# Second stage of a four-layer network: VectorE's range, spread, statistics and mean in another order

## The chip, the cores and the metric

The kernel runs on one core of a Trainium2 chip. The metric is the device time of one execution in microseconds, quoted as the median of several runs.

PE is TensorE (PEld its weight loads), DVE is VectorE, ACT is ScalarE, POOL is GpSimd and SP is the engine that issues transfers.

## The reference

Four layers, each `x = x + conv(groupnorm(x))`, on 8192 samples of 8 x 16 x 16. The second stage of the kernel is the end of layer 1 and the start of layer 2:

```python
# --- layer 1 ---
x = x + _L1_conv_ref(_gn(x), ...)      # ends with batch norm over all samples, then relu
# --- layer 2 ---
x = x + _L2_conv_ref(_gn(x), ...)      # starts with sx = 127 / max(abs(_gn(x))) over all samples
def _gn(v, G=4, eps=1e-5):
    ...
    m = jnp.mean(g, axis=(2, 3, 4), keepdims=True)
    s = jnp.var(g, axis=(2, 3, 4), keepdims=True)
    return ((g - m) / jnp.sqrt(s + eps)).reshape(v.shape)
```

Batch norm needs all of y first, and the quantizer of layer 2 needs the largest normalized value of all samples. Between the two stands a pass over 64 tiles of 128 x 2048 f32 (1.049 MB): load x and y, add relu(a y + b) to x, find the group statistics of each sample, subtract the mean, find the largest absolute value, store x again (but for the last ten tiles, which stay on chip).

## The kernel before

Engines that are wrapped in `InOrder` execute in the order of the program: `pe, dve, act, pool = (InOrder(tc, e) for e in (...))`. So the order of the calls in the last loop is the order of instructions on each engine.

```python
    def sums_pe(ps, x, sq):                       # PE: sums of x and of x*x over channels of a group
        for k, src in ((0, x), (1, sq)):
            for q in range(NQ):
                pe.matmul(ps[32 * q:32 * q + 32], L["wsum"][:, k], src[:, q * BANK:(q + 1) * BANK],
                          start=(k == 0), stop=(k == 1))
# ... cut ...
        def sum2(t):
            x, y = T[t]["x"], T[t].pop("y")
            act.activation(y, y, AF.Relu, bias=bn_b, scale=bn_a)
            pool.tensor_tensor(x, x, y, ALU.add)

        def sums2(t):                             # ACT, then PE
            sq = p2.tile([P, F], F32, name=f"sq2_{t}", tag="sq2", bufs=2)
            act.activation(sq, T[t]["x"], AF.Square)
            ps = ps2.tile([P, BANK], F32, name=f"gs_{t}", tag="gs")
            sums_pe(ps, T[t]["x"], sq)
            T[t]["ps"] = ps

        def stats2(t):                            # DVE: s_c, psc, gnst, sq_c, gnst; then POOL: power -0.5
            stats_small(gnst[:, t], psc[:, 32:64], T[t].pop("ps"), f"c{t}")
            stats_pow(gnst[:, t])

        def spread2(t):                           # DVE: diag_b, rows_c; then PE: gb
            ps = ps2.tile([P, 2, P], F32, name=f"gb_{t}", tag="gb")
            rows = to_rows(diag[t % 2], psc[:, 0:NQ], [gnst[:, t]], f"c{t}")
            for k, sel in enumerate((L["sel0"], L["sel1"])):
                pe.matmul(ps[:, k], sel, rows, start=True, stop=True)
            T[t]["gb"] = ps

        def centre2(t):                           # DVE: x - mean (mean in gb); then the store
            # ... two halves: x = x - gb[:, 0] ...
            if t >= NT - KEEP:
                kept[t] = x
            else:
                nc.sync.dma_start(x2_d[t], x)

        def range2(t):                            # DVE: max |x|, times 1/deviation (in gb), max
            # ... top = max |x| in two halves; top = top * gb[:, 1]; amax[:, t] = max(top) ...

        for t in range(NT + 3):
            on(t + 3, lambda t: t < 3 or load2(t))
            on(t, sum2)
            on(t - 2, spread2)
            on(t - 1, sums2)
            on(t - 3, range2)
            on(t - 2, centre2)
            on(t - 1, stats2)
```

The lines of the profile name the tiles of this loop. `gs` holds PE's sums and `s_c` is the first operation of the statistics, which reads them; `gnst` holds mean and 1/deviation; `diag_b` and `rows_c` are the two VectorE operations of the spread, and `gb` its result from PE; `top` belongs to the range. Below, PE's burst is its work for one tile without a pause: the spread of t-2, then the sums of t-1.

## Time and profile before

| | before |
|---|---|
| time, median of 3 | 4309.59 us (4309.05 to 4310.04) |
| the second stage (until the next stage's first VectorE work) | about 2985 to 3535 us |
| time per tile in it | 8.25 us |
| busy in 3100 to 3400: VectorE, PE, GpSimd | 83%, 55%, 67% |
| granted PE clock, DMA share, DMA rate there | 0.65, 1.00, 382 GB/s |

The page's table of 40 slices shows the stage as a hole in the PE row. Each digit is the busy share of one slice in tenths; a slice of the kernel before is 108 us long.

```profile
PE   6999999999999999999999999996555549999999
DVE  6666666666666666666666666655888879999997
PEclk9999999999999999999999999998666669999999
DMA  3222222222222222222222222114999933444442
```

In slices 29 to 32 PE falls to 5, its clock to 6 and DMA rises to 9, while VectorE is at 8. The stage is some 550 us, an eighth of the time.

### The profile page before, as it was taken

The page shows a single profiled execution, that of the slowest core. Times are in us where ns is not written, and L with a number is a line of the kernel's source. Part 1 is how long each engine was busy: PE and PEld are TensorE (multiplying, and loading weights), DVE is VectorE, ACT ScalarE, POOL GpSimd, SP SyncE. Part 2 cuts the span into 40 slices and gives each one's busy share as a digit, 9 for nine tenths or more (in the row PEclk, how much of TensorE's full clock was granted, in tenths as well). Part 3 has the DMA queues.
Part 4 walks back from the last instruction along what each step waited for, and adds up shares of the span by engine and source line. Part 5 has one row for each costly group of instructions (what it writes and reads, how often), then busy time and mean ns, then how long its engine had stood idle before and what let it go on. Part 6 is the DMA issues. An engine that isn't in the chain of part 4 may idle for free. (4 is left out here: it accounts for less than half of the span.)

```text
span 4309.0 us, 51166 instructions
## 1 busy us (share of the span) xinstructions
PE 3972.4 (92%) x19804; PEld 2087.4 (48%) x19866; DVE 3158.7 (73%) x4892; ACT 2153.1 (50%) x1606; POOL 2692.6 (62%) x1428
## 2 busy tenths in 40 slices
PE   6999999999999999999999999996555549999999
PEld 3555555555555555555555555553111115555555
DVE  6666666666666666666666666655888879999997
ACT  3444444444444444444444444443444437777776
POOL 5655546556555555455565565534666648999999
PEclk9999999999999999999999999998666669999999
DMA  3222222222222222222222222114999933444442
GB/s 116 88 98 80 106 88 88 108 79 88 108 79 94 103 80 102 94 88 108 79 89 108 79 90 106 69 52 171 391 382 382 382 123 137 176 186 186 176 186 108
DMA packets 80595, 587.26 MB, mean 136 GB/s; under 512 B 8928, under 2 KB 9056, under 8 KB 9184
## 3 DMA queue, kind: packets, MB, share of 16 engines
q1 hardware_dynamic: 80064, 583.04, 35.3%
q8 instruction: 156, 2.56, 0.2%
q10 hardware_dynamic: 288, 0.94, 0.1%
q14 instruction: 87, 0.71, 0.0%
HBM read 326.00 MB, written 257.95 MB: 136 GB/s over the span
## 5 line engine op out<-in xcount | busy, mean ns | idle before, releaser
L43 PE MATMUL po<-u,core 128*128 128x512 f32 x4096 | 1934.4, 608 | 0.0
L43 ACT COPY u<-pu 128x2048 f32<-128x2048 f32 x512 | 955.6, 1866 | 1052.3 <-PE pu L43 1052.3
L43 POOL TENSOR_TENSOR v<-x1n 128x256 f32<-128x256 f32 (+1 forms) x768 | 562.0, 761 | 907.1 <-issue 557.9
L43 PEld LDWEIGHTS po<-u,core 128*128 128x128 f32 x4096 | 722.8, 190 | 816.2 <-issue 815.2
L43 POOL TENSOR_TENSOR mvb<-mvb,mhalf 128x64 f32<-128x64 f32 (+1 forms) x67 | 676.1, 10093 | 127.4 <-DVE mvb L43 127.4
L43 PE MATMUL pu<-w,xn 32*128 32x256 f32 x8192 | 590.4, 402 | 11.3 <-DVE xn L43 9.3
L43 PEld LDWEIGHTS pu<-w,xn 32*128 32x128 f32 x8192 | 371.9, 185 | 311.7 <-issue 210.4
L43 ACT ACTIVATE sq<-x 128x2048 f32<-128x2048 f32 x192 | 366.2, 1907 | 268.8 <-POOL x L43 268.7
L43 DVE TENSOR_TENSOR x<-po,x 128x512 f32<-128x512 f32 x256 | 177.1, 692 | 420.0 <-PE po L43 412.4
L43 ACT ACTIVATE m<-pm,b 128x256 f32<-128x256 f32 x256 | 121.3, 474 | 591.7 <-PE pm L43 576.9
L43 DVE TENSOR_TENSOR y<-m,pm 128x256 f32<-128x256 f32 x512 | 192.9, 419 | 183.0 <-ACT m L43 183.0
L43 POOL TENSOR_TENSOR mv<-mv,mhalf 128x4 f32<-128x4 f32 x128 | 130.7, 1021 | 311.0 <-DVE mv L43 311.0
L43 POOL TENSOR_TENSOR x<-x,yl 128x2048 f32<-128x2048 f32 x64 | 290.6, 4540 | 10.5 <-ACT yl L43 10.4
L43 POOL TENSOR_TENSOR x<-x,w 128x2048 f32<-128x2048 f32 x64 | 289.9, 4531 | 11.4 <-DMA x<-in_xt 6.0
L43 PE MATMUL gb<-rows_c,sel 128*128 128x128 f32 x256 | 72.7, 436 | 237.8 <-DVE rows_c L43 237.8
L43 POOL TENSOR_TENSOR lo<-t,hi 128x2048 fp32r<-128x2048 f32 x64 | 273.4, 4272 | 19.4 <-POOL mv L43 16.2
L43 PE MATMUL pc<-v,fast 128*128 128x256 f32 x1024 | 275.3, 390 | 3.9 <-DVE y L43 3.9
L43 PE MATMUL pm<-v,fast 128*128 128x256 f32 x1024 | 264.8, 381 | 0.0
L43 PEld LDWEIGHTS pm<-v,fast 128*128 128x128 f32 x1024 | 195.1, 191 | 133.4 <-issue 118.6
L43 POOL TENSOR_TENSOR x<-x,c 128x2048 f32<-128x2048 f32 x64 | 236.6, 3697 | 0.0
L43 PE MATMUL pf<-hi,sign 128*128 128x512 f32 x768 | 226.9, 433 | 0.0
L43 PE MATMUL pf<-lo,sign 128*128 128x512 f32 x768 | 219.5, 423 | 3.4 <-ACT lo L43 3.4
(176 smaller groups left out, 5434.7 us busy)
## 6 DMA issues: line engine op xcount, KB each, us to landing
x_d<-x SPq DMA_DIRECT2D x118, 1024.0 KB, 4.7
x<-x_d SPq DMA_DIRECT2D x118, 1024.0 KB, 6.9
xb<-in_xb SPq DMA_DIRECT2D x64, 1024.0 KB, 4.8
x<-in_xt SPq DMA_DIRECT2D x64, 1024.0 KB, 4.8
y_d<-y SPq DMA_DIRECT2D x64, 1024.0 KB, 4.1
yl<-y_d SPq DMA_DIRECT2D x64, 1024.0 KB, 9.2
out_dram<-x SPq DMA_DIRECT2D x64, 1024.0 KB, 3.8
w<-in_pack ACTq DMA_DIRECT2D x1, 690.0 KB, 9.4
```

The costliest lines, as they stand in the source:

```text
L43: return self.tc.keep_in_program_order(op(*args, **kwargs))
```

## The change

The intent: in the kernel before, VectorE waits 1.13 us per tile for GpSimd's power, because the spread, which needs the power, follows the statistics, which start it, at once. With the mean and the range put between, the power should run unseen.

```diff
         for t in range(NT + 3):
             on(t + 3, lambda t: t < 3 or load2(t))
             on(t, sum2)
+            on(t - 3, range2)
             on(t - 2, spread2)
             on(t - 1, sums2)
-            on(t - 3, range2)
+            on(t - 1, stats2)
             on(t - 2, centre2)
-            on(t - 1, stats2)
```

## The prediction

> **What bounds the kernel now.** I read the page's 40 slices first: DMA is at 9 in only a few slices, and those are the stage that the change touches. So I cut that stage out with the table by windows. Its columns are the window and its length, then busy us (and instructions) of PE, PEld, DVE, ACT and POOL, then the granted PE clock, the DMA share and GB/s.
>
> ```profile
> core 0: us, PE busy (x) PEld busy (x) DVE busy (x) ACT busy (x) POOL busy (x), PEclk, DMA share, GB/s
> 3020.00:3040.00 20.00, 9.44 (x48) 2.67 (x40) 16.51 (x33) 11.00 (x6) 11.87 (x6) 0.74 1.01 422
> ...
> 3440.00:3460.00 20.00, 10.49 (x52) 3.08 (x44) 17.05 (x33) 10.45 (x6) 11.88 (x5) 0.67 1.00 387
> ...
> 3490.00:3500.00 10.00, 5.83 (x28) 1.53 (x20) 8.63 (x16) 5.34 (x3) 5.80 (x3) 0.67 0.00 0
> ```
>
> The reader is to see that DMA looks full (share 1.00) and still is not the bound. VectorE is 82 to 86% busy with the transfers (17.05 of 20; 16.51 of 20) and 86% without them (8.63 of 10, DMA share 0.00). The statistics' reduction s_c starts at 3194.54, 3202.79 and 3211.03 in mid-stage and at 3491.38, 3499.62 and 3507.87 after the last load: 8.25 us per tile both times. A tile moves 3 x 1.049 MB, which at 8.25 us is 381 GB/s; just after the start the same mix ran at 422. So the pace is a loop among engines. The timeline of one tile shows it (start, duration, engine, operation, and in brackets the idle time before):
>
> ```profile
> 3202.79 0.69 DVE L43 TENSOR_REDUCE s_c<-gs 128x32 f32<-128x512 f32 x1
> ...
> 3204.16 0.16 DVE L43 SCALAR_TENSOR_TENSOR gnst<-psc,sq_c 128x4 f32<-128x4 f32 x1
> 3204.40 1.02 POOL L43 TENSOR_TENSOR gnst<-gnst,mhalf 128x4 f32<-128x4 f32 x1 [2.72 <-DVE gnst L43]
> ...
> 3205.45 0.19 DVE L43 TENSOR_TENSOR diag_b<-gnst,psc 128x32 f32<-128x32 f32 x1 [1.13 <-POOL gnst L43]
> 3205.68 0.31 DVE L43 STREAM_TRANSPOSE rows_c<-diag_b 128x128 f32<-128x128 f32 x1
> 3205.91 2.30 DVE L43 TENSOR_REDUCE top<-x 128x64 f32<-128x1024 f32 x2
> ...
> 3206.14 1.19 PE L43 MATMUL gb<-rows_c,sel 128*128 128x128 f32 x4 [3.48 <-DVE rows_c L43]
> ...
> 3208.77 2.34 DVE L43 TENSOR_TENSOR x<-x,gb 128x1024 f32<-128x1024 f32 x2
> 3208.97 1.94 PE L43 MATMUL gs<-sq,wsum 128*32 128x512 f32 x8
> ...
> 3211.03 0.68 DVE L43 TENSOR_REDUCE s_c<-gs 128x32 f32<-128x512 f32 x1
> ```
>
> In start-to-start times the loop is: statistics with its gap 1.57 (3202.79 to 3204.36), wait for GpSimd's power 1.09, spread 0.46 (3205.45 to 3205.91), range 2.86 (to 3208.77), mean 2.26 (to 3211.03). The sum is 8.24. VectorE's only wait is the power; that is the wait the change aims at. The second thing to see is hidden: PE starts on the spread only when the rows are ready (3205.99), does the spread and then the sums for the next statistics, and ends at 3208.97 + 1.94 = 3210.91, just 0.12 before s_c starts. That run of matmuls is covered now by range and mean, 5.12 us of VectorE work, almost exactly its own length. The waits table of 3000 to 3500 says the same:
>
> ```profile
> PE gb L43 <- DVE rows_c L43: 223.3, 60, 4.3
> ...
> DVE diag_b L43 <- POOL gnst L43: 67.9, 60, 1.1
> DVE s_c L43 <- PE gs L43: 18.4, 2, 17.2
> ```
>
> VectorE waits for the power 60 times, and for PE's sums only twice, both at the stage's start.
>
> **What the Trainium skill says.** "TensorE: Matmul & The Clock Gate", section on the array's architectural detail (engine queue depths): VectorE, ScalarE and GpSimd queues are strict FIFO; PE may pull weight loads ahead, but, says the section on what happens when a matmul is issued, the matmuls keep program order. The trace agrees: in all 64 tiles the sums follow the spread, though their inputs were ready earlier (x of 3208's sums was added before 3197). The same page, part 1 on the clock gate: PE is at half clock until about 3.4 us of activity. The trace agrees: granted 0.50 in every window from 3197.2 to 3209, and the bursts (first gb to the end of the sums) take 4.76 us cold and 3.94 to 4.7 when the clock rises inside them; the mean of 64 is 4.52. "DMA: Bandwidth & Descriptors", section on where 436 GB/s comes from, gives about 358 GB/s as the limit of HBM per core; the trace differs, 381 sustained and 422 at the start, so I do not use that limit.
>
> **The change part by part.** No instruction is added or removed; per tile one order of VectorE work becomes another. Before: spread(t-2), range(t-3), mean(t-2), statistics(t-1). After: range(t-3), spread(t-2), statistics(t-1), mean(t-2). PE still has spread(t-2), then sums(t-1).
>
> 1. Gain: the power of t-1 now starts ahead of mean and range, 2.26 + 2.86 = 5.12 us of work that does not need it. GpSimd has finished the preceding addition long before (3201.68 against 3204.40). The 1.09 us wait goes.
> 2. Loss: between the rows of t-2 and the statistics of t-1 VectorE has nothing left in its program. The statistics need PE's sums, these stand behind the spread, and the spread needs the rows that VectorE has just made. The mean of t-2 could run after 1.2 us of spread, but stands behind the statistics in a FIFO. So VectorE waits for the full burst: handing over rows to PE 0.06 to 0.15 (the starts at 3008.26 and 3206.14 after rows ended at 3008.20 and 3205.99; I take 0.10), burst 4.52, PE's end to s_c 0.08 (3013.03 to 3013.11). That is 4.70.
> 3. New loop, all on the path: range 2.86 + diagonal and transpose to its end 0.54 + wait 4.70 + statistics 1.57 + mean 2.26 = 11.93 us, against 8.24. Net +3.69 per tile.
>
> The stage's start already has one such case: for the second tile nothing of range was there to cover PE, and rows ended at 3008.20, s_c came at 3013.11, 4.91 us later at cold clock.
>
> Whole stage: the second tile's statistics start at 3013.11 as now. The last (62 tiles on) start at 3013.11 + 62 x 11.93 = 3752.8. Then come statistics 1.57, mean 2.26, range 2.86, rows 0.54, last spread alone 0.10 + 0.70, mean 2.26, range 2.86, together 13.15: 3765.9. Before, the next stage began its first VectorE work at 3535.5. The difference is 230 us; before and after the stage nothing changes. 4309.6 + 230 = 4540.
>
> Other limits are far off at 11.93: GpSimd has 4.54 + 1.02, ScalarE 2.08 + 1.91 a tile, DMA 3.146 MB in 7.5 us at 422 GB/s. The centred tile is stored later in its turn, but loads are asked for three tiles ahead (36 us) and took a median of 9 to landing.
>
> **The rivals.**
> A. As intended: the power's wait goes and nothing replaces it. The loop falls to 7.15, but the stores and loads then need 7.45 at the start's 422 GB/s. 64 x (0.8 to 1.1) gives 50 to 70 us: 4240 to 4260, which is still within 2%. For it: the 60 waits of 1.13. Against: it needs sums(t-1) ready when VectorE asks, and PE's order forbids that.
> B. DMA is the bound (share 1.00), so nothing moves: 4310. Against: the same pace without DMA at 3490 to 3530. And even a DMA-bound stage would be overtaken by a loop of 11.9.
> C. PE's burst, now on the path, runs warm. At 3019.2 to 3021.2 the granted clock was 0.87 and eight sums took about 1.3 instead of 1.94. With spread at 0.7 and twice 1.3 less overlap the burst would be some 3.0, the loop 10.4: +135, 4445. Against: PE would idle 7.4 us a tile instead of 3.5, which does not keep a clock up. If instead every burst is cold (4.77), the loop is 12.18 and the time 4556.
>
> **Range and chances.** The main step is a chain of dependences, not a rate, so slower is nearly sure. The size hangs on the burst, between some 4.3 and 4.8, and on 0.1 us of handing over: 4540, with 4505 to 4575 for 8 in 10. Faster by over 2% (under 4223) is out of reach even for A: 0.01. Within 2% would need A or B: 0.03. Slower: 0.96.
>
> **What would show it.** Step 1: the wait of diag_b for the power vanishes from the waits table. Step 2: s_c waits for PE's gs some 60 times, about 4.7 each, near 290 us. Step 3: s_c of neighbouring tiles lie 11.9 apart, VectorE's share in the stage falls from 84% to about 58%, DMA's to near 265 GB/s (3.146 MB in 11.93 us), and the stage lasts some 230 us longer. The number of instructions and their durations stay. The prediction would be wrong if PE ran the sums ahead of the spread, if the burst ran warm (C), or if a wait I do not see, such as of the mean for the spread's buffers, came on top.

## The result, and the profile after

The changed kernel takes 4543.28 us (median of 4; 4542.78 to 4544.1) against 4309.82 for the kernel before beside it. The ratio is 1.0542 (95% interval 1.0523 to 1.056).

The waits of the changed kernel from 3000 to 3740 us (engine and tile that waited, what it waited for, us in total, times, longest):

```profile
PE gb L43 <- DVE rows_c L43: 452.5, 62, 7.4
...
DVE s_c L43 <- PE gs L43: 310.6, 62, 17.4
...
ACT yl L43 <- DMA yl<-y_d: 4.2, 3, 2.4
DVE diag_b L43 <- POOL gnst L43: 1.1, 1, 1.1
```

The wait that the change aimed at is gone: diag_b waits for GpSimd once in place of 60 times. In its place VectorE waits for PE's sums in every tile: without the first wait of 17.4 us, which the kernel before has too, 61 waits take 293 us, 4.81 each. The timeline of one tile shows the order that makes them:

```profile
3301.25 0.69 DVE L43 TENSOR_REDUCE s_c<-gs 128x32 f32<-128x512 f32 x1 [4.62 <-PE gs L43]
...
3302.71 2.35 DVE L43 TENSOR_TENSOR x<-x,gb 128x1024 f32<-128x1024 f32 x2
3302.87 1.02 POOL L43 TENSOR_TENSOR gnst<-gnst,mhalf 128x4 f32<-128x4 f32 x1 [6.26 <-DVE gnst L43]
...
3304.98 2.34 DVE L43 TENSOR_REDUCE top<-x 128x64 f32<-128x1024 f32 x2
...
3307.88 0.18 DVE L43 TENSOR_TENSOR diag_b<-gnst,psc 128x32 f32<-128x32 f32 x1
3308.09 0.31 DVE L43 STREAM_TRANSPOSE rows_c<-diag_b 128x128 f32<-128x128 f32 x1
...
3308.55 1.19 PE L43 MATMUL gb<-rows_c,sel 128*128 128x128 f32 x4 [7.37 <-DVE rows_c L43]
...
3311.38 1.94 PE L43 MATMUL gs<-sq,wsum 128*32 128x512 f32 x8
...
3313.38 0.69 DVE L43 TENSOR_REDUCE s_c<-gs 128x32 f32<-128x512 f32 x1 [4.98 <-PE gs L43]
```

The power (3302.87) now lies beside the mean and the range. But PE idles for 7.37 us until the rows are there, then works from 3308.55 to 3313.32 while VectorE stands still. The two engines take turns. The table by windows for 3100 to 3400 us, first of the kernel before, then of the changed kernel (columns as in the prediction):

```profile
3100.00:3400.00 300.00, 165.83 (x737) 53.70 (x736) 250.49 (x473) 140.60 (x73) 201.82 (x73) 0.65 1.00 382
```

```profile
3100.00:3400.00 300.00, 114.45 (x500) 38.11 (x500) 174.04 (x327) 97.36 (x50) 139.09 (x52) 0.57 0.77 263
```

VectorE falls from 250 to 174 of 300 us, DMA from 382 to 263 GB/s. The stages around it have not changed: the stage before it ends within 1 us of where it did, and the stage behind it lasts 773 us in both traces (3535.5 to 4309.0, and 3769.0 to 4542.3).

### The profile page after: what moved, and what is told of

Same layout as the page of the kernel before. It is cut to its first block, busy times and chain, and to the rows that moved or that the text cites. A ratio compares the mean times of both kernels' runs of the same rounds, so it can differ in the third digit from the quotient of the medians.

```text
span 4542.3 us, 51154 instructions
## 1 busy us (share of the span) xinstructions
PE 3977.7 (88%) x19804; PEld 2091.0 (46%) x19866; DVE 3159.2 (70%) x4892; ACT 2152.8 (47%) x1606; POOL 2691.0 (59%) x1428
## 5 line engine op out<-in xcount | busy, mean ns | idle before, releaser
L43 PEld LDWEIGHTS gb<-rows_c,sel 128*128 128x128 f32 x256 | 59.4, 322 | 565.3 <-issue 551.1
L43 POOL TENSOR_TENSOR gnst<-gnst,mhalf 128x4 f32<-128x4 f32 x64 | 65.2, 1019 | 407.7 <-DVE gnst L43 407.7
L43 DVE TENSOR_REDUCE s_c<-gs 128x32 f32<-128x512 f32 x64 | 44.3, 691 | 320.2 <-PE gs L43 320.2
```

Of the source, the lines that this page charges most:

```text
L43: return self.tc.keep_in_program_order(op(*args, **kwargs))
```

## The experiments

**Theory:** the order of the program exposes PE's burst (spread of t-2, then sums of t-1) between the rows and the statistics. In the kernel before, range and mean covered it. **First rival:** the mean now comes last in its turn, so the store comes late, and the transfers set the pace. For it speaks that a store of x took a median of 10.1 us to land in the stage after the change, and 4.8 before. **Second rival:** PE's granted clock fell from 0.65 to 0.57, and slow matmuls alone cost the time.

| run | VectorE's order, PE's order | time, us | ratio to before (95% interval) | per tile, us |
|---|---|---|---|---|
| before | spread, range, mean, statistics; spread, sums | 4310.9 | 1 | 8.25 |
| after | range, spread, statistics, mean; spread, sums | 4543.3 | 1.0542 (1.0523 to 1.056) | 11.95 |
| e1 | range, spread, mean, statistics; spread, sums | 4402.6 | 1.0213 (1.0196 to 1.023) | 9.72 |
| e2 | spread, range, statistics, mean; spread, sums | 4365.1 | 1.0125 (1.011 to 1.0141) | 9.10 |
| e3 | as after; sums, spread | 4250.2 | 0.9861 (0.9846 to 0.9875) | 7.29 |
| e4 | as before; sums, spread | 4310.6 | 0.9999 (0.9984 to 1.0014) | 8.24 |
| e5 | as after; spread twice, sums | 4579.9 | 1.0625 (1.0608 to 1.0643) | 12.54 |
| e6 | as before; spread twice, sums | 4329.0 | 1.0045 (1.003 to 1.006) | 8.53 |
| e7 | as after; spread, sums, 12 idle matmuls | 4604.6 | 1.0683 (1.0666 to 1.0701) | 12.80 |
| e8 | as after; spread, sums, 7 idle matmuls | 4416.1 | 1.0245 (1.0228 to 1.0263) | 9.90 |

The last column is the mean distance of the starts of s_c from the second tile to the last. All runs gave correct results. The time of "after" is from other rounds than e1 to e8; the kernel before had 4309.7 to 4310.9 us in all of them.

### e1: the range alone goes ahead

```diff
+            on(t - 3, range2)
             on(t - 2, spread2)
             on(t - 1, sums2)
-            on(t - 3, range2)
             on(t - 2, centre2)
             on(t - 1, stats2)
```

> One part of the change alone: the range of t-3 goes ahead of the spread of t-2, mean and statistics stay as before. Theory (VectorE's program must cover PE's burst of spread and sums): the wait for the power goes (range lies between), but only the mean, 2.26 us, and not range and mean, 5.12 us, is left to cover the burst. Loop = range 2.86 + rows 0.54 + (0.10 + burst 4.55 + 0.08) + statistics 1.57 = 9.60 us, against 8.25: 62 x 1.35 = +84 us, about 4394. Inside: the mean waits some 1.4 us for the spread, the statistics some 1.0 us for the sums. Rival (the late mean delays the stores and so the transfers, the mean stays early here): no loss, 4310 or less. Rival (less PE work per time lowers PE's clock and that alone costs): the same sign as the theory but no predicted size.

Measured: 4402.6 us and 9.72 us per tile, where 4394 and 9.60 were expected. VectorE in one tile:

```profile
3202.91 0.31 DVE L43 STREAM_TRANSPOSE rows_c<-diag_b 128x128 f32<-128x128 f32 x1
3204.66 2.35 DVE L43 TENSOR_TENSOR x<-x,gb 128x1024 f32<-128x1024 f32 x2 [1.43 <-PE gb L43]
3208.20 0.69 DVE L43 TENSOR_REDUCE s_c<-gs 128x32 f32<-128x512 f32 x1 [1.19 <-PE gs L43]
```

Both waits are those that were forecast: 1.43 us for the spread and 1.19 for the sums, 1.06 on average. The 0.12 us that are missing in the expected loop are the burst (mean 4.63, not 4.55) and the handing over from rows to PE (0.15, not 0.10). The mean is early here, and still the tile takes 1.5 us longer: the first rival does not explain this run.

### e2: the statistics alone go ahead of the mean

```diff
             on(t - 2, spread2)
             on(t - 1, sums2)
             on(t - 3, range2)
+            on(t - 1, stats2)
             on(t - 2, centre2)
-            on(t - 1, stats2)
```

> The other part alone: the statistics of t-1 go ahead of the mean of t-2, the range stays behind the spread. Theory: the power is covered by the mean (2.26 us), and the burst is covered by the range only (2.86 us). Loop = rows 0.54 + (0.10 + 4.52 + 0.08) + statistics 1.57 + mean 2.26 = 9.07 us: 62 x 0.82 = +51 us, about 4361. VectorE waits some 1.8 us per tile for the sums, none for the power. Rival (late mean delays the stores): the whole loss of the change shows here, about 4540, since the mean is as late as there.

Measured: 4365.1 us and 9.10 us per tile; VectorE waited 127 us for the sums in 63 waits, 2.02 each, and for the power once. The waits from 3000 to 3480 us, with the stage's first of 17.0 us:

```profile
DVE s_c L43 <- PE gs L43: 122.6, 53, 17.0
...
DVE diag_b L43 <- POOL gnst L43: 1.1, 1, 1.1
```

The mean comes as late here as in the changed kernel, and the time is 178 us lower: a late store is not the cause. The two parts alone cost 92 and 54 us, together 146, and the whole change 233. They do not add up, because both part runs save the same 1.09 us wait for the power, which can be saved only once: in us per tile, 1.47 + 0.85 + 1.09 = 3.41 of the 3.70. The remaining 0.3 is the slack of the kernel before. In the two part runs range and mean together hide 5.12 us, which is more than one burst with its handing over. The traces show the excess: PE's sums ended 0.38 us ahead of s_c on average in the kernel before, and 0.07 in the changed one, a difference of 0.31.

### e3: the change, with PE's sums ahead of the spread

```diff
             on(t - 3, range2)
-            on(t - 2, spread2)
             on(t - 1, sums2)
+            on(t - 2, spread2)
             on(t - 1, stats2)
             on(t - 2, centre2)
```

> The change with one swap on PE: sums of t-1 ahead of the spread of t-2 (range, sums, spread, statistics, mean). Theory: the sums need nothing of the rows, so PE can do them during range; the statistics find them done, the mean finds the spread done or nearly so. VectorE's loop is then its own work, 2.86 + 0.46 + 1.57 + 2.26 = 7.15 us, and the transfers may bind at 3.146 MB / 422 GB/s = 7.45 us: 62 x (7.45 - 8.25) = -50 us, about 4260 (4242 if DMA keeps up). s_c waits for PE no more. Rival (late mean, late stores): the mean is as late as in the change, so about 4540. Rival (PE's clock): PE has the same work, so no gain over the change of this size.

Measured: 4250.2 us, 293 us under the changed kernel and 61 under the kernel before. This is the fastest version. VectorE's order, with the mean behind the statistics, is that of the change to the last call. Two calls are swapped, and only PE sees it (ScalarE's square keeps its place). That settles the first rival. In the windows 3100 to 3200 and 3440 to 3460 of this run:

```profile
3100.00:3200.00 100.00, 61.33 (x272) 17.79 (x272) 95.07 (x182) 54.33 (x28) 75.32 (x29) 0.62 1.01 427
...
3440.00:3460.00 20.00, 11.99 (x60) 3.57 (x59) 19.33 (x36) 7.22 (x4) 12.06 (x5) 0.67 0.01 1
```

VectorE is 95% busy and DMA moves 427 GB/s, for which a tile's 3.146 MB take 7.37 us. Behind the last load the tiles follow each other in about 7.1 us, VectorE's own work, as the start-to-start sum of 7.15 said. In mid-stage both limits lie so close together that a tile takes between 7.0 and 8.7 us, and a load of x takes a median of 16.7 us to land (7.2 before). ScalarE waits 188 us in all for loads of y there (4.2 us in the kernel before). So the gain stops at the transfers.

### e4: the kernel before with PE's orders swapped, a control

```diff
-            on(t - 2, spread2)
             on(t - 1, sums2)
+            on(t - 2, spread2)
             on(t - 3, range2)
             on(t - 2, centre2)
             on(t - 1, stats2)
```

> Control: the kernel before with the same swap on PE alone, VectorE's order untouched. Theory: VectorE waits for the power, not for PE, so the loop stays 8.25 us and the time about 4310 (4300 to 4315). If PE's burst already set the pace before (it ends only 0.12 us ahead of the statistics), this would be faster by some tens of us.

Measured: 4310.6 us, no difference. In the kernel before, the power's wait sets the pace and PE's burst is covered; freeing PE alone gives nothing. Of the orders tried, only both edits together gain.

### e5 and e6: a dose of PE work in the burst

In both kernels each spread is computed twice, which lengthens the burst and changes no other instruction.

```diff
-            for k, sel in enumerate((L["sel0"], L["sel1"])):
-                pe.matmul(ps[:, k], sel, rows, start=True, stop=True)
+            for _ in range(2):
+                for k, sel in enumerate((L["sel0"], L["sel1"])):
+                    pe.matmul(ps[:, k], sel, rows, start=True, stop=True)
```

> Dose of PE's burst in the changed kernel: the two matmuls of every spread are issued twice (same result). One spread took 1.12 us to the first sum. Theory (burst stands openly between rows and statistics): +1.12 us in each of 63 loops, +71 us, about 4614; if the longer burst lets the clock rise inside it, less, down to some +45 us. VectorE's wait for the sums grows by the same amount. Rival (late mean and stores set the pace): nothing to +5 us, about 4545.

> The same dose in the kernel before. There range and mean cover 5.04 us from the end of the rows to the statistics; 0.10 + (4.52 + 1.12) + 0.08 = 5.82 us would be needed. Theory (the cover was nearly used up): the sums come 0.78 us late, +49 us, about 4360 (a rise of the clock inside the burst: down to +25 us), and a wait of the statistics for PE appears that the kernel before does not have. Rival (PE is far from mattering in the kernel before, 55% busy in the stage): about 4311, unchanged.

Measured: 4579.9 and 4329.0 us. Both signs are the theory's and both sizes are below the ranges that I gave: +37 us where at least +45 was expected, and +18 where at least +25 was. The dose was smaller than I thought. One tile of e5:

```profile
3310.01 2.04 PE L43 MATMUL gb<-rows_c,sel 128*128 128x128 f32 x8 [7.36 <-DVE rows_c L43]
3311.99 1.63 PE L43 MATMUL gs<-x,wsum 128*32 128x512 f32 x8
3313.44 1.03 PE L43 MATMUL gs<-sq,wsum 128*32 128x512 f32 x8
```

Two spreads take 1.98 us to the first sum, only 0.86 more than one; and in this longer burst the clock has risen when the last eight sums run (1.03 us in place of 1.94). The mean burst grew from 4.59 to 5.17 us, and 62 x 0.58 = 36 us is the loss that was measured. In e6 the mean burst is 4.90 and the tiles alternate: a burst of 4.40 gives 8.25 us per tile, one of 5.40 gives 8.82. So the cover of the kernel before ends at 5.40 - (8.82 - 8.25) = 4.83 us, and its cold burst of 4.76 was just inside. The wait of the statistics for PE that was forecast for e6 is there, behind every second tile: 31 waits of some 0.5 us, besides the one at the stage's start.

### e7 and e8: PE kept busy in its idle time

```diff
             sums_pe(ps, T[t]["x"], sq)
+            for _ in range(7):                       # 12 in e7
+                pe.matmul(idle, L["sel0"], core01.rearrange("p s n -> p (s n)")[:, 0:512], start=True, stop=True)
```

`idle` is a PSUM tile that nobody reads.

> How much of the open burst is the low clock: the changed kernel with twelve matmuls of 128x512 on constants behind each tile's sums, in PE's 7.4 us of idle time, into a bank nobody reads (the result is unchanged). At full clock they should take some 12 x 0.47 = 5.7 us (1934 us / 4096 in the first stage), so they end before the next rows. Theory (order exposes the burst, and idle time makes it cold): the granted clock rises towards 1.0, the burst falls from 4.59 to about 3.0 and the loop from 11.95 to about 10.4, 62 x 1.6 = 99 us less than the change: about 4445, and still 3% over the kernel before, because the order still exposes the burst. Rival (the low clock is the whole cause of the loss): back to about 4310. If the clock does not rise, the twelve matmuls take 11 us and the time rises well over 4543.

> As e7, with seven idle matmuls in place of twelve: in e7 each counted as two records and took 0.87 us at full clock, so twelve took 10.4 us and themselves filled the loop (12.80 us), while the granted clock rose to 1.00 and the burst fell to 2.46 us. Seven take 6.1 us and fit in the 7.4 us between the sums' end and the next spread. Theory: burst stays at 2.46, the loop is 2.86 + 0.54 + (0.10 + 2.46 + 0.08) + 1.57 + 2.26 = 9.87 us, 62 x 2.08 = 129 us under the change: about 4414, still 104 us (2.4%) over the kernel before. Rival (the low clock is the whole cause): about 4310. If 1.3 us of idle time per loop lets the clock fall again: near 4540.

e7 measured 4604.6 us. I had misread a count: an f32 matmul is two records in the trace, so twelve took 10.4 us and not 5.7, and they delayed the spread themselves. But PE ran at a granted clock of 1.00 and the burst fell to 2.46 us. e8 with seven measured 4416.1 us where 4414 was expected:

```profile
3301.48 6.28 PE L43 MATMUL idle<-core,sel 128*128 128x512 f32 x14
3308.92 0.68 PE L43 MATMUL gb<-rows_c,sel 128*128 128x128 f32 x4 [1.16 <-DVE rows_c L43]
3309.53 1.06 PE L43 MATMUL gs<-x,wsum 128*32 128x512 f32 x8
3310.42 1.04 PE L43 MATMUL gs<-sq,wsum 128*32 128x512 f32 x8
```

The burst is 2.54 us at clock 1.00, and VectorE still waits 2.75 us for the sums. So the second rival holds a part: the exposed burst alone costs 106 us at full clock (4416.1 - 4309.8), and the low clock, which comes from PE's idling, makes it 233. But the fall of the clock from 0.65 to 0.57 is not what costs it. The burst took 4.52 us on average in the kernel before already, and 4.59 after, which is 62 x 0.07 = 4 us. The change exposed a burst that was slow before. In e3 the clock is 0.62, lower than before, and it costs next to nothing: after the stage's start s_c waits for PE 10 us in all.

## Why the prediction was right

The prediction gave 4540 us and the measurement is 4543.3. Its terms in us per tile, with what the changed kernel shows for the tile above (the burst is the mean of 63):

| term | predicted | measured |
|---|---|---|
| range | 2.86 | 2.90 |
| diagonal and transpose | 0.54 | 0.52 |
| rows to PE | 0.10 | 0.15 |
| burst | 4.52 | 4.59 |
| PE's end to s_c | 0.08 | 0.06 |
| statistics to mean | 1.57 | 1.46 |
| mean | 2.26 | 2.27 |
| loop | 11.93 | 11.95 |

- **Gain (step 1):** right. One wait for the power is left in place of 60.
- **Loss (step 2):** right in mechanism and size: 4.81 us per wait where 4.70 was predicted. Two terms were off and cancelled: the handing over and the burst were 0.12 too small, and the statistics 0.11 too large. There the mean starts 0.08 us after the start of the last small operation (3302.63 to 3302.71), whose result it does not read.
- **Loop (step 3):** right. 62 loops make 62 x 3.71 = 230 us of the 233. Of the rest, 2.6 us are the stage's end (13.75 from the last s_c to the next stage, 11.14 before) and 1.1 its start: the stage before ended 0.96 us later in this profile.
- **The burst's mean** was taken from the kernel before, where it varied from 3.94 to 4.78. After the change it alternates between 4.39 and 4.77. The mean is almost the same, but I had no argument for that beyond PE's being idle in both; e7 shows that it could have been 2.46. That the size came out within 4 us is in this part luck.
- **Rival A** (gain of 50 to 70 us, stopped by the transfers) was not what the change does, but it is what e3 does: -61 us, at 427 GB/s. **Rival B** is refuted by 7.29 us per tile in e3: DMA was not the bound at 8.25. **Rival C** needed a PE that is kept busy; with that, in e8, the loop is 9.90, below the 10.4 that was forecast for a warm burst, because 2.54 us was less than the guessed 3.0.
- **The checks that it named:** VectorE's share about 58% (58.0%), DMA near 265 GB/s (263), the s_c waits near 290 us (293).
- **Misread, without effect on the result:** the x for the sums at 3207.26 and 3208.97 was not added before 3197 but from 3197.14 to 3201.68, and squared by 3203.63. It was ready before PE's spread all the same: in every tile but the first, the square was done at least 1.8 us before the sums began. The mean burst is one of 63, not of 64. VectorE's busy shares with the transfers are 83 and 85%, not 82 to 86.
- **The Trainium skill:** the strict FIFO of VectorE and PE's program order carried the whole argument, and every run agrees. For DMA I held about 358 GB/s to be what the page claims for this case and set it aside; the same page's "Measured" section has 425 GB/s for a single core, which e3's 427 meets.

Open: in the changed kernel the load of x waited for the landing of the tile before's store (435 us in all, by the transfer queue's waits), which it did not in the kernel before, and the store went out after the loads of the next tiles. No engine waited for it (ScalarE 4.2 us in the whole stage), so it cost nothing here; why it came to that was not tried.

## What to carry to other kernels

When an order hides a wait, write down for every pair "engine A hands to B, B hands back" how much independent work lies between, before and after; moving work into one gap takes it from another, and here a gap with 5.12 us of cover over a 4.7 us burst was emptied to fill one that needed 1.09. If two engines are in order, ask of the second one too what stands ahead of the result that you want: two swapped lines on PE turned the same VectorE order from 5.4% slower into 1.4% faster. Look at the clock at which an exposed burst runs: here PE idled in both orders, and the burst took some 1.8 times what it took with PE kept busy (4.59 against 2.46 to 2.54 us).

## What the Trainium skill lacked or had wrong

- "DMA: Bandwidth & Descriptors", section on where 436 GB/s comes from: it says that for HBM to SBUF the HBM side, some 358 GB/s, binds. Here loads and stores together ran at 427 GB/s for 300 us on a core alone (e3). The page's own "Measured" section has 425, for one core with its neighbour idle; the sentence on 358 does not repeat that condition.
- "TensorE: Matmul & The Clock Gate", part 1: that activity of about 3.4 us raises the clock fits the traces in size. In the changed kernel the granted share rose from 0.50 to 1.00 some 3.9 us into the burst from 3296.78, and not at all in the 4.77 us of the next one. What the page lacks are figures for a burst little longer than 3.4 us that comes back after idle time: the same work took 3.93 to 4.80 us from tile to tile, 2.46 us with PE busy throughout, and work put into the burst cost less than its own length (0.58 us for a second spread that takes 0.86). Idle time of 1.16 us in each 9.90 us kept the clock at 1.00 (e8).
- No page that I found says that an f32 matmul shows as two records in a trace (24 for twelve, e7). In a row at clock 1.00, one of 128x512 took 0.87 us (10.40 us for twelve from start to start), twice what I had read from one record.
- No page that I found gives a time for a power on GpSimd: 1.02 us for 128x4 f32, which is what the change set out to hide.
